# Graph layers on one core: 120 single-row tiles for 116, and the last two blocks normed in turn

## The chip, the cores and the metric

The kernel runs on one core of one Trainium2 chip. The metric is the device time of the whole program in microseconds (us), the median of several runs. One further execution is recorded by the hardware profiler; its own time and its span (first to last instruction of the program) are given beside each other.

## The reference

Two relational graph layers over 12,500 nodes of 128 floats and 200,000 edges sorted by destination, with eight relations, then a layer norm:

```python
W = jnp.einsum('rb,bio->rio', comp, basis)
msgs = einsum('ni,rio->nro', x, W)[src, et]
mean = segment_mean(msgs, dst * 8 + et)          # per node and relation
h = relu(mean.reshape(N, 8, 128).sum(1) + h @ root + bias) + h   # twice
out = layernorm(x + h)
```

## The kernel before

**Tiles.** The edges are cut into 1563 tiles of 128, and eight tiles make an octet: 196 octets per layer, the last with three tiles. The nodes are cut into 98 blocks of 128; the last, block 97, has 84. Blocks are normed in groups of eight, 13 groups; the last group holds the 212 nodes of blocks 96 and 97.

**Gathers and single rows.** For each tile, the 128 source rows are brought into SBUF. Most tiles take one indirect DMA issued by POOL (`gather`, L766). Some tiles, listed in `lists` (L647 to L653), take 128 DMAs of a single row each, issued by SP or ACT (`lone_rows`, L702), in chunks of 32; ahead of each chunk the queue loads 32 row addresses (L697). A list entry gives the queue, the first tile, the bound, the step, the chunk, the lead in octets and the hosts, the SBUF tiles that receive the rows and are used in turn. A chunk is emitted up to 15 octets ahead of its use. SP emits all chunks that are due, ACT at most one per octet.

**Layer 1.** Tables of messages for all nodes and relations lie in HBM as `y_d`. For each octet, in this order, the loop at the end emits the gathers (five octets ahead into seven row buffers), SP's and ACT's single rows, PE's matmuls `add_rows` (each tile's rows against its one-hot matrix, L1451, and for the first octet of a block the root term, L1454), DVE's `onehot` for the octet after next (L1188, two buffers), and one step of `todo`. From octet 190 on, the gather of an octet is emitted only two octets ahead and waits for PE's matmuls of the octet three before it (`LATE`, `after`). The order on each engine is the order of emission; every engine works its list in order, and waits are semaphores that the planner `Plan.add` derives from what is read and written. For a PSUM bank a read counts as a write.

**Blocks.** A block is summed in PSUM over the octets that hold its edges. `finish` adds what the block before it left over (L1360), makes the carry for the next block (L1364), and applies relu and residual into `wide` (L1383), with features on the partitions.

**Norm.** `norm(n)` puts ten steps into `todo`, one per octet: PE turns a group's blocks back to nodes on the partitions (L1511), DVE adds x (L1521) and takes statistics (L1527, L1530), ACT the square root (L1533), DVE the reciprocal (L1537, three octets later) and the scaling (L1540), and SP stores. ACT's square root stands on ACT behind the single-row chunks emitted before it.

**The end.** The last group is loaded as 106 partitions with two nodes each, so both of its slots need both blocks. In the last octet PE first puts x into two PSUM banks (`x_first`, L1485), then the root term (L1468), the carry (L1469) and the three tiles (L1471); then block 97 is finished, and `norm` turns both slots onto x (L1508), takes both statistics, one square root, one reciprocal and both scalings. SP and ACT each store a part. From octet 192 on, all pending norm steps are emitted within their octet.

Of the kernel before, what the change touches and what calls it, by code (L numbers as in the profile page):

```python
# [428 lines left out]
def ordered_path(  # L429
# [209 lines left out]
    def floats(t, n):  # L639
# [5 lines left out]
    mixer_f = mixer.rearrange("p m k -> p (m k)")  # L645
    idx_f = idx.bitcast(F32)
    lists = [  # L647
        [("SP", 90, 1552, 47, 32, 15, [(jmp.bitcast(F32), ["jmp"], []), (comp_sb, ["comp"], []),
                                     (sel.rearrange("p g k -> p (g k)"), ["sel"], [])]),
         ("ACT", 13 * Q + 2, 46 * Q, 8 * Q, 16, 10, [(floats(yr_f, j), yr_cells, yr_cells) for j in range(5)]),  # L650
         ("ACT", 53 * Q + 2, 1552, 8 * Q, 16, 10, [(floats(mixer_f, j), ["mixer"], []) for j in range(2)])],
        [("SP", 62, 1552, 49, 32, 15, [(floats(sT_f[0], j), [("sT", 0, 0), ("sT", 0, 1)], []) for j in range(4)]),
         ("ACT", 65, 1552, 50, 32, 15, [(floats(sT_f[1], j), [("sT", 1, 0), ("sT", 1, 1)], []) for j in range(4)])]]  # L653
    single, at_row = [{}, {}], [0, 0]
    for l in range(L):
        for k, (_, t0, t1, by, _, _, hosts) in enumerate(lists[l]):
# [562 lines left out]
    def in_rows(a, n):  # L1219
        p, k = shape_of(n)  # L1220
        return a[n * GN:n * GN + p * k, :].rearrange("(p s) d -> p (s d)", s=k)

    def load_x(n):
        if n >= NX:
            return
        p, k = shape_of(n)
        t, c = xs[n] = xg_r.take()
        load(t[:p, :k, :].rearrange("p s d -> p (s d)"), in_rows(x, n), [], [c])

    def by_slot(t, n):  # L1230
# [3 lines left out]
    def turn_x(n, h):  # L1234

        p, k = shape_of(n)
        pt, pc = pt_b
        m = min(4, k)

        def first_step():  # L1240
            t, c = xs[n]
            if h == 0:
                xT[n] = wide_r.take()

            def emit():
                for s in range(m):
                    last = nc.tensor.transpose(pt[:, s, :p], t[:p, 4 * h + s, :], ident[:p, :p])
                return last

            pe(emit, [c, "ident"], [pc])  # L1250

        def second_step(copy=copy):
            o, oc = xT[n]
            copy(by_slot(o, n)[:, 4 * h:4 * h + m, :], pt[:, :m, :p], [pc], [oc + (h,)])

        return first_step, second_step
# [175 lines left out]
             (s_b[1][0].rearrange("p t d -> p (t d)")[:, :2 * P], s_b[1][1]),  # L1432
             (ct_b[0].rearrange("p t d -> p (t d)")[:, :2 * P], ct_b[1])]

    def add_rows(q, k, opens, last):
        t, c = rows_g.pop((1, q))
        d, dc = dms.pop((1, q))
        a, ac = acc[k]
        n = in_quad(q)
        root_in = opens and k >= 0  # L1440
        more = []
        if root_in:
            ht, hc = hT[:, k * P:k * P + rows_of(k)], ("h", k)
            more += [hc, ("w", 1, R)]

        lones = lones_of(1, q)

        def some(i0, i1):
            def emit():
                for i in range(i0, i1):  # L1450
                    ins = nc.tensor.matmul(a, lones[i][0] if i in lones else t[:, i, :], d[:, i, :],  # L1451
                                           start=(opens and i == 0), stop=(last and i == n - 1 and q != SOON // Q))
                    if i == 0 and root_in:
                        nc.tensor.matmul(a[:, :rows_of(k)], w_sb[:, 1, R, :], ht, start=False, stop=False)  # L1454
                if q == SOON // Q:
                    ins = nc.tensor.matmul(a, fix_rows, fix_dm, start=False, stop=last)
                return ins

            return emit

        if q == NQ - 2:
            for h in range(2):
                pe(some(4 * h, 4 * h + 4), [c + (h,)] + dc + more, [ac, ("done", 1)])
        elif q == NQ - 1:
            m = rows_of(k)
            assert opens and last and k == NT - 1
            ct, cc = carry.pop(k)
            pe(lambda: nc.tensor.matmul(a[:, :m], w_sb[:, 1, R, :], ht, start=True, stop=False), more, [ac])  # L1468
            pe(lambda: nc.tensor.matmul(a[:, :m], ident, ct[:, :m], start=False, stop=False), [cc, "ident"], [ac])  # L1469
            for i in range(n):  # L1470
                pe(lambda i=i: nc.tensor.matmul(a[:, :m], t[:, i, :], d[:, i, :m], start=False, stop=i == n - 1),  # L1471
                   [c + (i,)] + dc, [ac, ("done", 1)])
        else:
            pe(some(0, n), [c + (0,), c + (1,)] + dc + more + [x for _, cs in lones.values() for x in cs]
               + (fix_rows_c + fix_dm_c if q == SOON // Q else []),
               [ac, ("done", 1)])
        plan.mark("PE")

    def x_first():
        n = NX - 1  # L1480
        p, k = shape_of(n)
        xt, xc = xs[n]
        assert k == 2
        for s, (b, bc) in enumerate(po_b):
            pe(lambda s=s, b=b: nc.tensor.matmul(b[:p, 0, :], ident[:p, :p], xt[:p, s, :], start=True, stop=False),  # L1485
               [xc, "ident"], [bc])

    def norm(n):

        p, k = shape_of(n)  # L1490
        vt, vc = wide[n]
        xt, xc = xs[n]
        st, sc = st_r.take()
        A, M = nc.vector.BN_STATS_DIM, nc.vector.BN_AGGR_DIM
        z = xt[:p]
        on_x = n == NX - 1
        y = [b[:p, 0, :] for b, _ in po_b] if on_x else [z[:, s, :] for s in range(k)]
        yc = [c for _, c in po_b] if on_x else [xc + (0,)]
        halves = [(h, min(4, k - 4 * h)) for h in range(-(-k // 4))]

        def turn():
            for h, m in halves:
                b, bc = po_b[h]

                def emit(h=h, m=m, b=b):
                    for s in range(m):
                        if on_x:
                            last = nc.tensor.matmul(po_b[s][0][:p, 0, :], by_slot(vt, n)[:, s, :], ident,  # L1508
                                                    start=False, stop=True)
                        else:  # L1510
                            last = nc.tensor.transpose(b[:p, s, :], by_slot(vt, n)[:, 4 * h + s, :], ident)  # L1511
                    return last

                pe(emit, [vc + (j,) for j in range(n * S, min(n * S + S, NT))] + ["ident"],
                   [c for _, c in po_b] if on_x else [bc])

        def add():
            for h, m in [] if on_x else halves:
                b, bc = po_b[h]
                zh = z[:, 4 * h:4 * h + m, :]  # L1520
                vec(lambda b=b, m=m, zh=zh: nc.vector.tensor_add(zh, b[:p, :m, :], zh), [bc, xc], [xc + (0,)])  # L1521

        def each(f):
            return in_turn([lambda s=s: f(s) for s in range(k)])

        def stats():
            vec(each(lambda s: nc.vector.bn_stats(st[:p, s, :A], y[s])), yc, [sc + (0,)])  # L1527

        def aggr():
            vec(each(lambda s: nc.vector.bn_aggr(st[:p, s, A:A + M], st[:p, s, :A])), [sc + (0,)], [sc + (1,)])  # L1530

        def root_of():
            act(lambda: nc.scalar.activation(st[:p, :k, A + M], st[:p, :k, A + 1], AF.Sqrt, bias=eps[:p]),  # L1533
                [sc + (1,), "eps"], [sc + (2,)])

        def one_by():
            vec(lambda: nc.vector.reciprocal(st[:p, :k, A + M], st[:p, :k, A + M]), [sc + (2,)], [sc + (3,)])  # L1537

        def scale():
            vec(each(lambda s: nc.vector.tensor_scalar(z[:, s, :], y[s], st[:p, s, A:A + 1], st[:p, s, A + M:],  # L1540
                                                       op0=ALU.subtract, op1=ALU.mult)),
                [sc + (1,), sc + (3,)] + (yc + [xc] if on_x else []), [xc + (0,)])

        def store():
            cut = p // 16 * 16
            for q, p0, p1 in (("SP", 0, cut), ("ACT", cut, p)):
                if p1 > p0:
                    load(in_rows(out, n)[p0:p1], xt[p0:p1, :k, :].rearrange("p s d -> p (s d)"), [xc + (0,)],
                         [("out", n, q)] + ([xc] if p0 == 0 else []), q)

        todo.extend([turn, add, stats, aggr, root_of, lambda: None, lambda: None, one_by, scale, store])
# [223 lines left out]
    for q in range(NQ):  # L1775
# [11 lines left out]
        if opens:  # L1787
            acc[k] = acc_b[k % 3]
        if q == NQ - 1:
            x_first()  # L1790
        add_rows(q, k, opens, last)
        onehot(1, q + 2)
        if todo:
# [1 line left out]
        for i in range(2):  # L1795
            for j, step in ending:
                step()
                n = j // S
                if j >= 0 and (j % S == S - 1 or j == NT - 1):
                    norm(n)  # L1800
                    if n + 2 < NX:
                        todo.extend([lambda: None] * 3 + [lambda n=n: load_x(n + 2)])
            ending.clear()
            if i == 0 and last:
                a, b = finish(1, k)
                a()
                ending.append((k, b))
# [69 lines left out]
```

## Time and profile before

| | |
|---|---|
| median of 3 runs | 3784.03 us (3783.49 to 3790.35) |
| profiled execution | 3783.55 us, span 3781.7 us |
| granted TensorE clock, mean | 0.83 |
| busy: PE / DVE / ACT / POOL | 2413.2 / 1694.7 / 354.0 / 2844.7 us |
| gathers, layer 0 / layer 1 | 1508 / 1502 |
| single-row DMAs, layer 1, SP / ACT | 3968 / 3840 |

Issuing DMAs isn't counted as busy, so ACT's and SP's work on single rows shows in timelines and not in the busy times. A line of a timeline gives start, duration (merged over several instructions where it has a count), engine, line, operation, tiles, count, and in brackets the idle time before it and what ended it. "SPq" and "ACTq" are DMA issues of these engines.

### The profile page before, as it was taken

The page shows a single profiled execution, that of the slowest core. Times are in us where ns is not written, and L with a number is a line of the kernel's source. Part 1 is how long each engine was busy: PE and PEld are TensorE (multiplying, and loading weights), DVE is VectorE, ACT ScalarE, POOL GpSimd, SP SyncE. Part 2 cuts the span into 40 slices and gives each one's busy share as a digit, 9 for nine tenths or more (in the row PEclk, how much of TensorE's full clock was granted, in tenths as well). Part 3 has the DMA queues.
Part 4 walks back from the last instruction along what each step waited for, and adds up shares of the span by engine and source line. Part 5 has one row for each costly group of instructions (what it writes and reads, how often), then busy time and mean ns, then how long its engine had stood idle before and what let it go on. Part 6 is the DMA issues. An engine that isn't in the chain of part 4 may idle for free.

```text
span 3781.7 us, 62930 instructions
## 1 busy us (share of the span) xinstructions
PE 2413.2 (64%) x11367; PEld 1933.4 (51%) x11367; DVE 1694.7 (45%) x4752; ACT 354.0 (9%) x794; POOL 2844.7 (75%) x3019
## 2 busy tenths in 40 slices
PE   5777667777666676777765555556566555655655
PEld 3566645555555555665543444444444444444444
DVE  5556424444333333343344444444444444454444
ACT  1121211211111111111100000000000000000000
POOL 7777777777777777777777777777777777777776
PEclk8999879999888888788888787777777777787778
DMA  4122223433322222223232222222222222222222
GB/s 125 56 62 62 56 92 102 123 111 101 99 87 81 89 89 84 84 82 96 92 85 55 56 62 61 65 63 61 66 56 67 66 56 67 60 62 67 67 54 61
DMA packets 155888, 286.71 MB, mean 76 GB/s; under 512 B 67013, under 2 KB 89474, under 8 KB 155482
## 3 DMA queue, kind: packets, MB, share of 16 engines
q0 software_dynamic: 96352, 197.52, 20.3%
q10 hardware_dynamic: 30461, 55.51, 4.5%
q1 hardware_dynamic: 28669, 29.60, 3.0%
q14 instruction: 314, 2.57, 0.2%
q8 instruction: 92, 1.51, 0.2%
HBM read 223.72 MB, written 58.65 MB: 75 GB/s over the span
## 4 chain that ended last, share of the span: by engine, by line
POOL 52%; issue 19%; DMA 11%; PE 9%; ACTq 4%; ACT 2%; DVE 2%; SPq 2%; POOLq 0%; DVEq 0%
POOL rows L766 52%; DMA rows<-y_d,idy 9%; ACTq L702 3%; PE s L1276 2%; PE s L1451 1%; SPq L702 1%; ACT sT L623 1%; ACTq L697 1%; PE y L1308 1%; DVE dm L1188 1%; PE pt L1406 1%; PE ct L959 1%; PE ct L960 1%; DVE arena L949 1%; PE pt L907 1%
## 5 line engine op out<-in xcount | busy, mean ns | idle before, releaser
L766 POOL DMA_INDIRECT rows<-in_x_dram,idx x1508 | 1425.2, 945 | 462.4 <-issue 455.7
L766 POOL DMA_INDIRECT rows<-y_d,idy x1502 | 1417.4, 944 | 458.5 <-issue 446.9
L1188 DVE TENSOR_SCALAR dm<-cols,near,w 128x256 f32<-128x256 f16 x1563 | 723.8, 534 | 952.1 <-PE s L1451 570.3
L1451 PE MATMUL s<-dm,rows 128*128 128x256 f32 x1984 | 659.9, 495 | 447.7 <-DMA rows<-y_d,idy 349.0
L1451 PEld LDWEIGHTS s<-dm,rows 128*128 128x128 f32 x1984 | 491.9, 257 | 580.2 <-issue 316.9
L1188 DVE TENSOR_SCALAR dm<-cols,kr,w 128x128 f32<-128x128 f16 x1563 | 524.9, 400 | 201.8 <-PE s L1276 177.5
L1276 PEld LDWEIGHTS s<-dm,rows 128*128 128x128 f32 x3016 | 436.3, 225 | 291.7 <-DMA rows<-in_x_dram,idx 243.0
L1276 PE MATMUL s<-dm,rows 128*128 128x128 f32 x3016 | 462.1, 313 | 189.0 <-DMA rows<-in_x_dram,idx 182.3
L1451 PE MATMUL ct<-dm,rows 128*128 128x256 f32 x1014 | 341.9, 501 | 294.2 <-DMA rows<-y_d,idy 281.4
L1451 PEld LDWEIGHTS ct<-dm,rows 128*128 128x128 f32 x1014 | 255.3, 262 | 364.2 <-issue 234.5
L1308 PE MATMUL y<-w_sb,sT 128*128 128x128 f32 x1968 | 270.1, 296 | 55.8 <-ACT sT L623 55.8
L1308 PEld LDWEIGHTS y<-w_sb,sT 128*128 128x128 f32 x1968 | 257.0, 211 | 64.6 <-ACT sT L623 63.6
L1406 PE MATMUL pt<-w_sb,arena 128*128 128x512 f32 (+1 forms) x386 | 222.5, 660 | 62.3 <-DVE y_row L626 42.3
L1339 PE MATMUL po<-pl,ys 128*128 128x256 f32 x392 | 138.4, 437 | 140.8 <-ACT sT L623 135.9
L623 ACT ACTIVATE sT<-s 128x512 f32<-128x512 f32 x391 | 213.5, 606 | 83.7 <-PE s L1276 83.4
L626 DVE COPY y_row<-pt 128x512 f32<-128x512 f32 x56 | 38.7, 691 | 364.6 <-PE pt L1406 364.6
L623 ACT ACTIVATE y_row<-pt 128x512 f32<-128x512 f32 (+1 forms) x139 | 83.0, 597 | 1041.7 <-PE s L1276 574.3
L1308 PE MATMUL ct<-w_sb,sT 128*128 128x128 f32 (+1 forms) x1168 | 159.8, 296 | 0.7 <-ACT sT L623 0.7
L1308 PEld LDWEIGHTS ct<-w_sb,sT 128*128 128x128 f32 (+1 forms) x1168 | 155.0, 213 | 1.3 <-ACT sT L623 1.1
L1533 ACT ACTIVATE st<-st,eps 128x8 f32<-128x8 f32 (+1 forms) x13 | 4.0, 308 | 1586.5 <-DMA sT<-y_d 736.9
L1339 PEld LDWEIGHTS po<-pl,ys 128*128 128x128 f32 x392 | 65.2, 201 | 169.0 <-ACT sT L623 159.0
L1360 DVE TENSOR_TENSOR po<-po,carry 128x128 f32<-128x128 f32 x98 | 29.0, 296 | 263.8 <-PE s L1276 242.7
(210 smaller groups left out, 1296.9 us busy)
## 6 DMA issues: line engine op xcount, KB each, us to landing
sT<-y_d SPq DMA_DIRECT2D x3968, 0.5 KB
sT<-y_d ACTq DMA_DIRECT2D x3840, 0.5 KB
y_d<-y_row ACTq DMA_DIRECT2D x96, 512.0 KB
mixer<-in_x_dram ACTq DMA_DIRECT2D x2304, 0.5 KB
rows<-in_x_dram,idx POOLq DMA_INDIRECT x1508
rows<-y_d,idy POOLq DMA_INDIRECT x1502
jmp<-in_x_dram SPq DMA_DIRECT2D x1408, 0.5 KB
comp_sb<-in_x_dram SPq DMA_DIRECT2D x1408, 0.5 KB
```

Of the source, the lines that this page charges most:

```text
L623: act(lambda: nc.scalar.activation(out_t, in_t, AF.Copy), reads, writes)
L626: vec(lambda: nc.vector.tensor_copy(out_t, in_t), reads, writes)
L697: _, at = nc.values_load_multi_w_load_instructions(offs[r:r + 1, l * P + j * ch:l * P + (j + 1) * ch], engines=[mybir.EngineType.SP if e = ...
L702: return [eng.dma_start(o[j * ch + i:j * ch + i + 1, :].bitcast(byte), table_b[bass.ds(v, 4 * D)].rearrange("(p d) -> p d", p=1)) for i, v ...
L766: ins.append(nc.gpsimd.indirect_dma_start(out=t[:, i - q * Q, :], out_offset=None, in_=table_t, in_offset=bass.IndirectOffsetOnAxis(ap=ids ...
L907: last = nc.tensor.matmul(pt[:, b, :], t[:, b, :], m, start=(i == 0), stop=(i == len(parts) - 1))
L1188: emits.append(lambda i=i: nc.vector.tensor_scalar(t[:, i - q * Q, :wide], cols[:, :wide], ids[:, i:i + 1], w[:, i:i + 1], op0=ALU.is_equa ...
L1276: last = nc.tensor.matmul(s_b[i // 4][0][:, i % 4, :], lones[i][0] if i in lones else t[:, i, :], d[:, i, :], start=True, stop=True)
L1308: last = nc.tensor.matmul(y[:m], t[:, r, :nt, :].rearrange("p t k -> p (t k)"), w_sb[:, 0, r, :], start=(r == 0), stop=(r == R - 1))
L1339: ins = nc.tensor.matmul(a, o[:m], t[:m], start=opens, stop=last and not root_in)
L1406: pe(lambda: nc.tensor.matmul(hb[:n].rearrange("p r d -> p (r d)"), hT[:, j * P:j * P + n], w_sb[:, 1, k * H:(k + 1) * H, :].rearrange("p ...
L1451: ins = nc.tensor.matmul(a, lones[i][0] if i in lones else t[:, i, :], d[:, i, :], start=(opens and i == 0), stop=(last and i == n - 1 and ...
```

## The change

- The lists of single-row tiles have other starts and steps: layer 0, SP from tile 91 every 45 (before: 90 every 47); layer 1, SP every 47 (49) and ACT from tile 63 every 48 (65 every 50).
- The last group's two slots are its two blocks: block 96 on 128 partitions, block 97 on 84. x for it is loaded by two DMAs, and turned and copied per block.
- Ahead of octet 194, PE puts x of both blocks into PSUM and the root term of block 97 into its bank (`first_sums`). In octet 195 PE sums tiles 0 and 1, turns block 96 onto x, adds the carry and sums tile 2.
- Block 96 is finished in the order add, relu and residual, carry. The two blocks are normed by `last_norm`, one after the other, their steps interleaved on DVE; block 96 is stored by SP, block 97 by ACT.

```diff
-        [("SP", 90, 1552, 47, 32, 15, [(jmp.bitcast(F32), ["jmp"], []), (comp_sb, ["comp"], []),
+        [("SP", 91, 1552, 45, 32, 15, [(jmp.bitcast(F32), ["jmp"], []), (comp_sb, ["comp"], []),
...
-        [("SP", 62, 1552, 49, 32, 15, [(floats(sT_f[0], j), [("sT", 0, 0), ("sT", 0, 1)], []) for j in range(4)]),
-         ("ACT", 65, 1552, 50, 32, 15, [(floats(sT_f[1], j), [("sT", 1, 0), ("sT", 1, 1)], []) for j in range(4)])]]
+        [("SP", 62, 1552, 47, 32, 15, [(floats(sT_f[0], j), [("sT", 0, 0), ("sT", 0, 1)], []) for j in range(4)]),
+         ("ACT", 63, 1552, 48, 32, 15, [(floats(sT_f[1], j), [("sT", 1, 0), ("sT", 1, 1)], []) for j in range(4)])]]
...
+        if n == NX - 1:
+            for s, (j, p) in enumerate(ends_at):
+                load(t[:p, s, :], x[j * P:j * P + p, :], [], [c])
+            return
...
-            pe(lambda: nc.tensor.matmul(a[:, :m], w_sb[:, 1, R, :], ht, start=True, stop=False), more, [ac])
-            pe(lambda: nc.tensor.matmul(a[:, :m], ident, ct[:, :m], start=False, stop=False), [cc, "ident"], [ac])
             for i in range(n):
+                if i == n - 1:
+                    between_last()
+                    pe(lambda: nc.tensor.matmul(a[:, :m], ident, ct[:, :m], start=False, stop=False),
+                       [cc, "ident"], [ac])
                 pe(lambda i=i: nc.tensor.matmul(a[:, :m], t[:, i, :], d[:, i, :m], start=False, stop=i == n - 1),
...
+    def first_sums():
+        xt, xc = xs[NX - 1]
+        for i, ((_, p), (b, bc)) in enumerate(zip(ends_at, po_b)):
+            pe(lambda i=i, p=p, b=b: nc.tensor.matmul(b[:p, 0, :], ident[:p, :p], xt[:p, i, :], start=True, stop=False),
                [xc, "ident"], [bc])
+        k = NT - 1
+        a, ac = acc[k] = acc_b[k % 3]
+        m = rows_of(k)
+        pe(lambda: nc.tensor.matmul(a[:, :m], w_sb[:, 1, R, :], hT[:, k * P:k * P + m], start=True, stop=False),
+           [("h", k), ("w", 1, R)], [ac])
...
+    def last_norm(i):
...
+        def turn():
+            pe(lambda: nc.tensor.matmul(y, vt[:, i * P:i * P + p], ident, start=False, stop=True),
+               [vc + (j,), "ident"], [bc])
+        def stats():
+            vec(lambda: nc.vector.bn_stats(t[:, :A], y), [bc], [sc + (i, 0)])
+            vec(lambda: nc.vector.bn_aggr(t[:, A:A + M], t[:, :A]), [sc + (i, 0)], [sc + (i, 1)])
+            act(lambda: nc.scalar.activation(t[:, A + M:], t[:, A + 1:A + 2], AF.Sqrt, bias=eps[:p]),
+                [sc + (i, 1), "eps"], [sc + (i, 2)])
+        def one_by():
+            vec(lambda: nc.vector.reciprocal(t[:, A + M:], t[:, A + M:]), [sc + (i, 2)], [sc + (i, 3)])
+        def scale():
+            vec(lambda: nc.vector.tensor_scalar(z, y, t[:, A:A + 1], t[:, A + M:], op0=ALU.subtract, op1=ALU.mult),
+                [sc + (i, 1), sc + (i, 3), bc, xc], [xc + (i,)])
+            load(out[j * P:j * P + p, :], z, [xc + (i,)], [("out", NX - 1, i)], ("SP", "ACT")[i])
...
         if q == NQ - 1:
-            x_first()
+            last_st = st_r.take()
+            turn, stats, one_by, scale = zip(*(last_norm(i) for i in range(2)))
+            add_rows(q, k, opens, last, turn[0])
+            stats[0]()
+            for step in finish(1, k):
+                step()
+            turn[1]()
+            one_by[0]()
+            stats[1]()
+            scale[0]()
+            one_by[1]()
+            scale[1]()
+            break
+        if q == NQ - 2:
+            first_sums()
         add_rows(q, k, opens, last)
...
-            if i == 0 and last:
+            if q == NQ - 2:
+                if i == 0:
+                    for step in finish(1, k, True):
+                        step()
+            elif i == 0 and last:
```

More of the change, by code (lines that the diff above doesn't have):

```diff
@@ L1221, in in_rows @@
         return a[n * GN:n * GN + p * k, :].rearrange("(p s) d -> p (s d)", s=k)
+    ends_at = [(j, rows_of(j)) for j in range((NX - 1) * S, NT)]
+    assert len(ends_at) == 2
     def load_x(n):
@@ L1246, in emit @@
                 for s in range(m):
-                    last = nc.tensor.transpose(pt[:, s, :p], t[:p, 4 * h + s, :], ident[:p, :p])
+                    r = ends_at[s][1] if n == NX - 1 else p
+                    last = nc.tensor.transpose(pt[:, s, :r], t[:r, 4 * h + s, :], ident[:r, :r])
                 return last
@@ L1253, in second_step @@
             o, oc = xT[n]
+            if n == NX - 1:
+                for s, (_, r) in enumerate(ends_at):
+                    copy(o[:, s * P:s * P + r], pt[:, s, :r], [pc], [oc + (s,)])
+                return
             copy(by_slot(o, n)[:, 4 * h:4 * h + m, :], pt[:, :m, :p], [pc], [oc + (h,)])
@@ L1433, in ordered_path, with add_rows @@
              (ct_b[0].rearrange("p t d -> p (t d)")[:, :2 * P], ct_b[1])]
-    def add_rows(q, k, opens, last):
+    def add_rows(q, k, opens, last, between_last=None):
         t, c = rows_g.pop((1, q))
@@ L1477, in add_rows @@
         plan.mark("PE")
[L1479 to L1485, printed above, removed]
-               [xc, "ident"], [bc])
+    def first_sums():
+        xt, xc = xs[NX - 1]
+        for i, ((_, p), (b, bc)) in enumerate(zip(ends_at, po_b)):
+            pe(lambda i=i, p=p, b=b: nc.tensor.matmul(b[:p, 0, :], ident[:p, :p], xt[:p, i, :], start=True, stop=False),
+               [xc, "ident"], [bc])
+        k = NT - 1
[4 more added lines that the diff above has]
+    def last_norm(i):
+        j, p = ends_at[i]
+        xt, xc = xs[NX - 1]
+        vt, vc = wide[NX - 1]
+        st, sc = last_st
+        b, bc = po_b[i]
+        y, z = b[:p, 0, :], xt[:p, i, :]
+        A, M = nc.vector.BN_STATS_DIM, nc.vector.BN_AGGR_DIM
+        t = st[:p, i, :]
+        def turn():
[12 more added lines that the diff above has]
+            load(out[j * P:j * P + p, :], z, [xc + (i,)], [("out", NX - 1, i)], ("SP", "ACT")[i])
+        return turn, stats, one_by, scale
     def norm(n):
@@ L1495, in norm @@
         z = xt[:p]
-        on_x = n == NX - 1
-        y = [b[:p, 0, :] for b, _ in po_b] if on_x else [z[:, s, :] for s in range(k)]
-        yc = [c for _, c in po_b] if on_x else [xc + (0,)]
         halves = [(h, min(4, k - 4 * h)) for h in range(-(-k // 4))]
@@ L1506, in emit @@
                     for s in range(m):
[L1507 to L1511, printed above, removed]
-                    return last
-                pe(emit, [vc + (j,) for j in range(n * S, min(n * S + S, NT))] + ["ident"],
-                   [c for _, c in po_b] if on_x else [bc])
+                        last = nc.tensor.transpose(b[:p, s, :], by_slot(vt, n)[:, 4 * h + s, :], ident)
+                    return last
+                pe(emit, [vc + (j,) for j in range(n * S, min(n * S + S, NT))] + ["ident"], [bc])
         def add():
-            for h, m in [] if on_x else halves:
+            for h, m in halves:
                 b, bc = po_b[h]
@@ L1526, in stats @@
         def stats():
-            vec(each(lambda s: nc.vector.bn_stats(st[:p, s, :A], y[s])), yc, [sc + (0,)])
+            vec(each(lambda s: nc.vector.bn_stats(st[:p, s, :A], z[:, s, :])), [xc + (0,)], [sc + (0,)])
         def aggr():
@@ L1539, in scale @@
         def scale():
-            vec(each(lambda s: nc.vector.tensor_scalar(z[:, s, :], y[s], st[:p, s, A:A + 1], st[:p, s, A + M:],
+            vec(each(lambda s: nc.vector.tensor_scalar(z[:, s, :], z[:, s, :], st[:p, s, A:A + 1], st[:p, s, A + M:],
                                                        op0=ALU.subtract, op1=ALU.mult)),
-                [sc + (1,), sc + (3,)] + (yc + [xc] if on_x else []), [xc + (0,)])
+                [sc + (1,), sc + (3,)], [xc + (0,)])
         def store():
@@ L1798, in ordered_path @@
                 n = j // S
-                if j >= 0 and (j % S == S - 1 or j == NT - 1):
+                if j >= 0 and j % S == S - 1:
                     norm(n)
```

## The prediction

> **What bounds the kernel now.** I read the chain of waits first, then the source view of the gather line, then the timelines of the queues that the moved rows go to, and last the tail.
>
> ```profile
> span 3781.7 us, 62930 instructions
> POOL 52%; issue 19%; DMA 11%; PE 9%; ACTq 4%; ACT 2%; DVE 2%; SPq 2%; POOLq 0%; DVEq 0%
> L766 POOL DMA_INDIRECT rows<-in_x_dram,idx x1508: 940/944/1177, 4.6 to 1888.9; - x189
> L766 POOL DMA_INDIRECT rows<-y_d,idy x1502: 940/944/1009, 1890.2 to 3768.1; - x188
>   issue: 902.6, 2957
>   PE s L1451: 3.4, 11
> ```
>
> POOL starts its first gather at 4.6 and its last at 3768.1, and the two layers follow each other without a gap (1888.9, then 1890.2). That is 3010 gathers in 3763.5 us, 1.250 us each: 0.944 busy, the rest almost all "issue" (902.6 us over 2957 gathers, 0.305 each). Waits for another engine are hardly there (3.4 us for PE). So POOL is the bound and a gather is worth 1.25 us. This holds as long as what POOL waits for stays early, and two things can make it late: the row buffers, and the last six octets, whose gathers are held until PE has done the octet three before.
>
> **Part 1: four gathers less.** The ranges in the lists give 33 + 5 + 18 = 56 single-row tiles in layer 0 (55 before) and 32 + 32 = 64 in layer 1 (61 before). So the change does what it says: one gather less in layer 0, three in layer 1. The first moves the start of layer 1, the others its end, one for one: 4 x 1.250 = 5.0 us. The nearest row with another price is busy time alone, 0.944: 3.8 us. I take 5.0, since "issue" goes away with its gather.
>
> **Part 2: what the 4 x 128 rows cost on the queues.** In layer 1 both queues are in the way of other work, ACT above all, because the square root of every normalisation (L1533) stands in its order behind 32-row chunks.
>
> ```profile
> 1913.76 269.62 ACTq L702 DMA_DIRECT2D sT<-y_d  x640
> 2183.40 1.28 ACT L1533 ACT_TABLE_LOAD   x1 [277.08 <-DMA sT<-y_d]
> L702 ACTq DMA_DIRECT2D sT<-y_d x1344: 231/240/584, 2199.9 to 2799.3; - x192
> 2469.83 156.59 ACTq L702 DMA_DIRECT2D sT<-y_d  x352
> 2773.06 150.01 ACTq L702 DMA_DIRECT2D sT<-y_d  x352
> 3211.08 137.95 ACTq L702 DMA_DIRECT2D sT<-y_d  x320
> 3362.38 130.62 ACTq L702 DMA_DIRECT2D sT<-y_d  x320
> 3522.62 102.46 ACTq L702 DMA_DIRECT2D sT<-y_d  x256
> 3661.18 0.31 ACT L1533 ACTIVATE st<-st,eps 128x8 f32<-128x8 f32 x1 [140.54 <-DVE dm L1188]
> 2185.04 0.21 DVE L1537 RECIPROCAL st<-st 128x8 f32<-128x8 f32 x1 [15.35 <-ACT st L1533]
> 2340.52 0.20 DVE L1537 RECIPROCAL st<-st 128x8 f32<-128x8 f32 x1 [24.78 <-ACT st L1533]
> ```
>
> ACT issues without a pause: 640 DMAs are 20 chunks in 269.62 us, 13.5 us each. From 2199.9 to 2799.3 it is 42 chunks in 599.4, 14.3 each with the square roots between them. Later, with about 2.3 us added for the gap after each square root: 152.3/11 = 13.8, 140.3/10 = 14.0, 132.9/10 = 13.3, 104.8/8 = 13.1. So ACT is late early on, and DVE's reciprocal waits 15.35 and 24.78 us for it at the first two normalisations. Before the end it has caught up: at 3661.18 ACT waited for DVE, not the reverse.
>
> With a tile every 48 instead of every 50, ACT never catches up. I count chunks in emission order. Ahead of the first square root are 21 (20 now), ahead of the second 32 (31), ahead of the eleventh, that of blocks 80 to 87, all 128 (120 now). The eleventh is reached at 1913.76 - 1.25 + 269.62 x 21/20 + 1.3 = 2196.9, plus 107 chunks. At 42 x 14.3 + 65 x 13.7 (the four later rates have a mean of 13.6) that is 2196.9 + 600.6 + 890.5 = 3688; with 14.0 for the last 65, the slower of those rates, 3707. I take both as the ends of the likely case.
>
> ```profile
> 3688.65 0.20 DVE L1537 RECIPROCAL st<-st 128x8 f32<-128x8 f32 x1
> 3694.90 3.71 DVE L1188 TENSOR_SCALAR dm<-cols,near,w 128x256 f32<-128x256 f16 x8 [5.85 <-PE ct L1451]
> 3709.55 5.38 PE L1451 MATMUL s<-dm,rows 128*128 128x256 f32 x16 [4.36 <-DMA rows<-y_d,idy]
> 3768.10 0.94 POOL L766 DMA_INDIRECT rows<-y_d,idy  x1 [0.31 <-issue]
> ```
>
> DVE will ask for it at 3688.65 - 5 = 3683.7, so it waits some 5 to 24 us. Queued behind it on DVE is the one-hot of octet 188 (3.71 us), behind that PE's 16 passes of that octet (5.38), and behind PE's octet 188 stand POOL's gathers of octet 191, one of the last six. These start naturally 33 gathers before the last: 3768.1 - 5.0 - 33 x 1.249 = 3721.9. So the square root may come as late as 3721.9 - 5.4 - 3.7 - about 0.8 of hops = 3712 and cost nothing; past that, POOL loses one for one. My 3688 to 3707 lies 5 to 24 us inside. The earlier waits are longer (about 40 us at the second) but there POOL runs ahead into seven row buffers, and PE normally trails it by under two octets: some five octets of (3768.1 - 1890.2)/195 = 9.6 us, 48 us of cover, besides the two one-hots that DVE has built before it waits. I cost them at nothing; without that cover each would cost its excess. The rows themselves come in time: the last tile ACT loads (1551, octet 193) is issued before 3707, and that octet's matmuls come after 3750.
>
> SP has more room: its 128 rows take about 53 us (below, 768 in 317.10) against 45 gathers of 1.25 = 56. In layer 0 its list is also still shorter than its period, and nothing stalls. The last group of x is loaded by two DMAs to one cell, so the second waits on SP for the first, twice in the kernel, a few us each, with no row due behind it.
>
> ```profile
> 1913.58 317.10 SPq L702 DMA_DIRECT2D sT<-y_d  x768
> ```
>
> **Part 3: the tail.** In order of time:
>
> ```profile
> 3764.36 3.31 DMA rows<-y_d,idy
> 3767.71 3.55 PE L1451 MATMUL s<-dm,rows 128*128 128x256 f32 x8 [2.53 <-DMA rows<-y_d,idy]
> 3771.05 0.77 PE L1485 MATMUL po<-x_g,ident 106*106 106x128 f32 x4
> 3771.29 0.30 DVE L1360 TENSOR_TENSOR s<-s,carry 128x128 f32<-128x128 f32 x1 [5.71 <-PE s L1451]
> 3771.66 0.35 PE L1468 MATMUL s<-arena,w_sb 128*128 128x84 f32 x2
> 3771.88 0.29 DVE L1383 SCALAR_TENSOR_TENSOR wide<-s,arena 128x128 f32<-128x128 f32 x1
> 3771.90 0.45 PE L1469 MATMUL s<-carry,ident 128*128 128x84 f32 x2
> 3772.19 0.83 PE L1471 MATMUL s<-dm,rows 128*128 128x84 f32 x6
> 3773.06 0.24 DVE L1383 SCALAR_TENSOR_TENSOR wide<-s,arena 128x84 f32<-128x84 f32 x1 [0.89 <-PE s L1471]
> 3773.36 0.69 PE L1508 MATMUL po<-ident,wide 128*106 128x128 f32 x4 [0.34 <-DVE wide L1383]
> 3774.09 0.50 DVE L1527 BATCH_NORM_STATS2 st<-po 106x6 f32<-106x128 f32 x2 [0.78 <-PE po L1508]
> 3774.62 0.25 DVE L1530 BATCH_NORM_AGGREGATE st<-st 106x2 f32<-106x6 f32 x2
> 3774.90 0.30 ACT L1533 ACTIVATE st<-st,eps 106x2 f32<-106x2 f32 x1 [13.09 <-DVE st L1530]
> 3775.23 0.17 DVE L1537 RECIPROCAL st<-st 106x2 f32<-106x2 f32 x1 [0.37 <-ACT st L1533]
> 3775.44 0.73 DVE L1540 TENSOR_SCALAR x_g<-po,st 106x128 f32<-106x128 f32 x2
> 3776.20 0.34 ACTq L620 DMA_DIRECT2D out_dram<-x_g  x1
> ```
>
> The x and root passes (0.77 + 0.35) go to PE's idle time of 2.53 us before 3767.71: free. But the last pass does not come 1.1 us earlier, because the carry now comes after the relu of block 96 on DVE. On today's clock: add 3771.29, relu to 3771.92, carry to 3772.3; block 96 into PSUM 3771.98 to 3772.35; carry pass, last tile's passes, to 3772.98. Now it is 3773.02: nothing gained. From there one block is normed instead of two slots: relu 0.24, one slot's pass 0.36, stats 0.27, aggregate 0.20, root 0.30, reciprocal 0.17, scale 0.38, seven hops of about 0.03: 2.15, against 3776.20 - 3773.02 = 3.18. Block 96's own stats and scale lie in DVE's waits for PE and ACT. Gain about 1.0 us; none if they do not fit there (they are 0.27 + 0.20 + 0.17 + 0.38 = 1.0), 1.3 if DVE's instructions overlap more. The last store and what follows it, 3781.7 - 3776.2 = 5.5, stays.
>
> **The sum.** The profiled execution took 3783.55 us (span 3781.7). 3783.55 - 5.0 - 1.0 = 3777.55. The median of the runs shown, 3784.03, is 0.48 above it: 3778.0, or 0.16% less. About 0.2% (7.6 us: 3776.5 to 3791.6) is what a measurement of this kernel can tell from no change.
>
> **The rivals.**
> - *ACT's square root becomes the bound.* If the pace of 2469.83 ((156.59 + 2.3)/11 = 14.44 a chunk) lasts the whole layer, the eleventh is reached at 2196.9 + 107 x 14.44 = 3742, 30 us past 3712, and POOL stands for them at octet 191: 3808, slower. It decides from 14.16 a chunk on; each 0.1 beyond costs 10.7. For it: the stretch to 2799 held 14.3, and the two lists are now denser. Against: the first 20 chunks and all after 2773 were quicker. The Trainium skill ("DMA: Bandwidth & Descriptors", section "Issuing engines are not separate DMA queues") says that DMAs of the scalar, sync and gpsimd engines run on the same 16 DMA engines and interleave; by that rule the added rows hinder each other and the gathers, which speaks for this rival, and DMA_DIRECT2D's spread of 231/240/584 ns agrees.
> - *The same, mildly:* 14.16 to 14.29 a chunk, up to 13 us lost: 3779 to 3791, no change.
> - *The tail gains nothing* (block 96's steps push block 97's): 3779.0, no change.
> - *More than counted:* 1.3 in the tail and a quieter DMA side: 3776, just faster.
>
> **How the numbers follow.** Forecast, with the tail as summed or without gain (3776.5 to 3779.5): 0.68. Mild delay: 0.12. ACT the bound by more than 13 us: 0.12. More than counted: 0.08. The range reaches from 3775.7 (1.3 in the tail, and a run's scatter of 1) to 3789, which takes in most of the mild delay. Faster 0.08, same 0.80, slower 0.12.
>
> **What would show it.** Right: 1507 and 1499 gathers in the gather line, the last starting near 3763.1 with no wait on PE; DVE's reciprocals waiting 20 to 45 us for ACT in the first half and less at the eleventh; the last out store some 6 us earlier. Wrong: a gap of POOL in the 3720s released by PE, with the eleventh square root after 3712; or a tail in which block 97's statistics wait for block 96's scale.

## The result and the profile after

Over 20 runs each, the changed kernel takes 3776.43 us in the median (3775.01 to 3778.68), the kernel before 3783.14: 6.7 us less, a ratio of 0.9984 with a 95% interval of 0.9978 to 0.9990. That lies inside the range of 3775.7 to 3789 and within the 0.2% counted as no change, though the interval is narrow enough to say that it is a little faster.

The page of after (its span, and the shares of the chain):

```profile
span 3774.6 us, 63987 instructions
POOL 41%; issue 17%; DMA 14%; PE 9%; ACTq 8%; SPq 4%; ACT 3%; DVE 2%; POOLq 0%; DVEq 0%
```

and the gather line in its source view, with POOL's idle time by "issue" below:

```profile
L766 POOL DMA_INDIRECT rows<-in_x_dram,idx x1507: 940/944/1264, 4.7 to 1887.4; - x189
L766 POOL DMA_INDIRECT rows<-y_d,idy x1499: 940/944/1047, 1888.7 to 3762.4; - x188
  issue: 899.1, 2945
```

3006 gathers for 3010, at the same busy time and the same "issue" each. The last starts at 3762.4 instead of 3768.1: 5.7 us, of which four gathers are 5.0. The chain now has ACTq and SPq at 8% and 4% (4% and 2% before) and POOL at 41% (52%): POOL still sets the pace, but the queues with the single rows now lie on the chain for part of the time.

The timelines of ACT and of DVE, around the normalisations (the first two lines are the second, the others the eleventh):

```profile
2350.10 0.31 ACT L1571 ACTIVATE st<-st,eps 128x8 f32<-128x8 f32 x1 [154.78 <-DMA sT<-y_d]
2350.44 0.21 DVE L1575 RECIPROCAL st<-st 128x8 f32<-128x8 f32 x1 [34.91 <-ACT st L1571]
3694.79 3.71 DVE L1188 TENSOR_SCALAR dm<-cols,near,w 128x256 f32<-128x256 f16 x8 [6.46 <-PE ct L1463]
3705.12 0.31 ACT L1571 ACTIVATE st<-st,eps 128x8 f32<-128x8 f32 x1 [158.54 <-DMA sT<-y_d]
3705.46 0.21 DVE L1575 RECIPROCAL st<-st 128x8 f32<-128x8 f32 x1 [6.97 <-ACT st L1571]
```

The eleventh square root came at 3705.12, directly behind ACT's own row issues. In the waits of the whole span (total, number, longest), DVE's reciprocal waits 244.9 us for ACT in 12 waits; before it was 40.9 in 4. The idle time of POOL has no wait for PE above 0.3 us, the length of its usual gap:

```profile
POOL rows L766 <- issue: 899.1, 2945, 0.3
POOL rows L766 <- PE s L1463: 1.5, 5, 0.3
DVE st L1575 <- ACT st L1571: 244.9, 12, 34.9
```

The tail, in order of time:

```profile
3762.41 0.94 POOL L766 DMA_INDIRECT rows<-y_d,idy  x1 [0.30 <-issue]
3764.94 0.30 DVE L1372 TENSOR_TENSOR s<-s,carry 128x128 f32<-128x128 f32 x1 [2.13 <-PE s L1463]
3765.28 0.29 DVE L1395 SCALAR_TENSOR_TENSOR wide<-s,arena 128x128 f32<-128x128 f32 x1
3765.60 0.35 DVE L1402 TENSOR_SCALAR carry<-s,bias_t 128x128 f32<-128x128 f32 x1
3765.62 0.49 PE L1515 MATMUL po<-ident,wide 128*128 128x128 f32 x2 [0.31 <-DVE wide L1395]
3766.30 0.39 PE L1485 MATMUL s<-dm,rows 128*128 128x84 f32 x2
3766.72 0.25 DVE L1395 SCALAR_TENSOR_TENSOR wide<-s,arena 128x84 f32<-128x84 f32 x1
3767.51 0.29 DVE L1519 BATCH_NORM_STATS2 st<-po 84x6 f32<-84x128 f32 x1 [0.32 <-PE po L1515]
3767.84 0.18 DVE L1520 BATCH_NORM_AGGREGATE st<-st 84x2 f32<-84x6 f32 x1
3767.94 0.38 DVE L1528 TENSOR_SCALAR x_g<-po,st 128x128 f32<-128x128 f32 x1
3768.05 0.29 ACT L1521 ACTIVATE st<-st,eps 84x1 f32<-84x1 f32 x1 [1.06 <-DVE st L1520]
3769.01 0.35 ACTq L620 DMA_DIRECT2D out_dram<-x_g  x1
```

From the last gather's start to the last store's issue it is 6.60 us, before 8.10. Block 96's scaling (3767.94) lies beside block 97's square root, as the change's order on DVE intends. From the store to the end it is 5.6 us (5.5 before).

### The profile page after: what moved, and what is told of

Read it like the earlier page. It is cut to its first block, busy times and chain, and to the rows that moved or that the text cites. A ratio compares the mean times of both kernels' runs of the same rounds, so it can differ in the third digit from the quotient of the medians.

```text
span 3774.6 us, 63987 instructions
## 1 busy us (share of the span) xinstructions
PE 2394.9 (63%) x11367; PEld 1919.0 (51%) x11367; DVE 1692.9 (45%) x4754; ACT 354.4 (9%) x795; POOL 2840.8 (75%) x3015
## 4 chain that ended last, share of the span: by engine, by line
POOL 41%; issue 17%; DMA 14%; PE 9%; ACTq 8%; SPq 4%; ACT 3%; DVE 2%; POOLq 0%; DVEq 0%
POOL rows L766 41%; DMA rows<-y_d,idy 12%; ACTq L702 6%; SPq L702 4%; ACTq L697 2%; PE s L1288 2%; ACT sT L623 2%; PE y L1320 1%; PE pt L1418 1%; ACT y_row L623 1%; SPq L697 1%; PE s L1463 1%; DVE dm L1188 1%; PE ct L959 1%; PE ct L960 1%
## 5 line engine op out<-in xcount | busy, mean ns | idle before, releaser
L1463 PE MATMUL s<-dm,rows 128*128 128x256 f32 x1984 | 627.9, 478 | 444.7 <-DMA rows<-y_d,idy 328.2
L1463 PEld LDWEIGHTS s<-dm,rows 128*128 128x128 f32 x1984 | 472.5, 247 | 569.9 <-issue 305.8
L1288 PEld LDWEIGHTS s<-dm,rows 128*128 128x128 f32 x3014 | 435.9, 225 | 273.6 <-DMA rows<-in_x_dram,idx 222.7
L1463 PE MATMUL ct<-dm,rows 128*128 128x256 f32 x1008 | 357.4, 521 | 305.0 <-DMA rows<-y_d,idy 190.1
L1463 PEld LDWEIGHTS ct<-dm,rows 128*128 128x128 f32 x1008 | 265.7, 274 | 379.2 <-issue 202.8
```

The costliest lines, as they stand in the source:

```text
L1288: last = nc.tensor.matmul(s_b[i // 4][0][:, i % 4, :], lones[i][0] if i in lones else t[:, i, :], d[:, i, :], start=True, stop=True)
```

## The experiments

**A series on a chip where the queues are slow.** The first four kernels ran together, beside the kernel before, on a chip on which the kernel before itself took 5790.47 us. There was no other series on that chip, so whether the chip or the moment was slow is not shown.

Lists alone: the kernel before with

```diff
-        [("SP", 90, 1552, 47, ...
+        [("SP", 91, 1552, 45, ...
...
-        [("SP", 62, 1552, 49, ...
-         ("ACT", 65, 1552, 50, ...
+        [("SP", 62, 1552, 47, ...
+         ("ACT", 63, 1552, 48, ...
```

> The kernel before with the new lists of single-row tiles alone; its tail is the old one. Theory (a gather of POOL is worth 1.25 us, ACT's lateness stays hidden): 4 x 1.25 = 5.0 us under the kernel before, 3778.1, last gather starting near 3763, DVE's reciprocals waiting about 245 us in all for ACT as in the changed kernel. Rival 1 (the gain is the tail's): 3783, no change. Rival 2 (the added rows slow the gathers too, so less than 1.25 each): 3779 to 3782.

Tail alone: the changed kernel with these three entries as before.

> The changed kernel with the old lists of single-row tiles; only the tail is new. Theory: last gather at 3768 as before, and from there to the last store's issue about 6.6 instead of 8.1 us, of which about 0.9 is the norm and the rest PE's clock in octet 194 (chance): 1.0 us under the kernel before, 3782.1. Rival (the tail gives the whole 1.5): 3781.6. Rival 2 (the tail gives the whole change): 3776.4.

Sums late: `first_sums()` moved from ahead of octet 194 to the start of octet 195.

```diff
         if q == NQ - 1:
...
+            first_sums()
             add_rows(q, k, opens, last, turn[0])
...
-        if q == NQ - 2:
-            first_sums()
```

> The changed kernel, but x and the root term enter PSUM in the last octet, after octet 194, as before the change. Theory: PE's 1.1 us then stand between octet 194 and the last tiles, where PE otherwise waits about 0.5 us for DVE's relu: 0.6 us over the changed kernel, 3777.0. Rival 1 (the carry on DVE sets the end anyway): 3776.4. Rival 2 (all of it counts): 3777.5.

Reciprocal later:

```diff
-        todo.extend([turn, add, stats, aggr, root_of, lambda: None, lambda: None, one_by, scale, store])
+        todo.extend([turn, add, stats, aggr, root_of, lambda: None, lambda: None, lambda: None, lambda: None, lambda: None, one_by, scale, store])
...
-                        todo.extend([lambda: None] * 3 + [lambda n=n: load_x(n + 2)])
+                        todo.extend([lambda: None] * 2 + [lambda n=n: load_x(n + 2)])
```

> The changed kernel with the reciprocal of each norm put five instead of two octets after the square root (and the load of x one octet earlier after the store). Theory (DVE's 245 us of waits for ACT are hidden by the row buffers): the waits fall by some 20 to 29 us each, to under 60 in all, and the time does not move, 3776.4 within 1 us. Rival (part of these waits reaches the end): faster by 2 us or more.

| kernel | median | ratio to the kernel before |
|---|---|---|
| lists alone | 5925.49 | 1.0232 (1.0203 to 1.0261) |
| tail alone | 5782.61 | 0.9990 (0.9972 to 1.0008) |
| sums late | 5926.34 | 1.0243 (1.0216 to 1.0270) |
| reciprocal later | 5922.05 | 1.0230 (1.0208 to 1.0252) |

None of the four expectations fits. All three with the new lists are 2.3 to 2.4% slower, the one with the old lists is not. Lists alone, the chain on its page:

```profile
SPq 60%; issue 35%; another core or an unknown queue 2%; PE 1%; DVE 1%; ACTq 1%; DMA 0%; ACT 0%; DVEq 0%
```

the gather line of layer 0 in the source view, with what POOL waited for in both layers:

```profile
L766 POOL DMA_INDIRECT rows<-in_x_dram,idx x1507: 938/944/1157, 4.7 to 2809.9; - x189
  PE s L1276: 746.7, 80
  PE s L1451: 520.3, 21
  PE ct L1451: 474.4, 16
```

what PE waited for in layer 1, in the waits view:

```profile
PE ct L1451 <- DMA sT<-y_d: 709.5, 15, 56.8
PE s L1451 <- DMA sT<-y_d: 660.5, 15, 54.6
```

the rows of SP:

```profile
L702 SPq DMA_DIRECT2D sT<-y_d x4096: 2/228/1407, 2863.6 to 5860.6; - x196
L702 SPq MOVE sT<-y_d x4096: 2/29/1412, 2863.5 to 5860.5; - x196
```

and the same rows of SP in the changed kernel on the usual chip:

```profile
L702 SPq DMA_DIRECT2D sT<-y_d x4096: 224/228/623, 1911.3 to 3696.9; - x196
L702 SPq MOVE sT<-y_d x4096: 29/29/29, 1911.3 to 3696.8; - x196
```

There SP takes (5860.6 - 2863.6)/4096 = 0.73 us for a row of layer 1, and in the changed kernel on the usual chip 0.44 by the same quotient. Medians of the single instructions are equal, but even a register move of 29 ns takes up to 1412. So SP is the bound, POOL waits for PE and PE for rows, and a tile given to SP costs 128 x 0.73 = 94 us in layer 1 instead of saving 1.25. Tail alone, with the old lists, has SPq at 59% and issue at 36% of its chain on that chip, so SP bounds the old lists there too. The new lists give SP one tile more in each layer. In layer 0 a row took (2792.0 - 123.4)/4224 = 0.63 us, so that tile is 81; with the 94 of layer 1 that makes 175 us. 135 came out. By the last gathers of the two traces (2727.9 and 5766.0 with tail alone, 2809.9 and 5900.1 with lists alone), layer 0 took 82 us more and layer 1 only 52; why less there is not shown. Why the queues pause was not studied.

**The same four on a usual chip**, again in one series; there the kernel before took 3781.80.

> The same kernel as rows_only (old tail, new lists), measured again beside the kernel before. If the kernel before takes about 3783 us, POOL is the bound and the theory says 4 x 1.25 = 5.0 us less, 3778. If it takes about 5790 us again, SP is the bound (two more SP tiles of some 94 us of issue each, less what was slack) and it is again some 2.3% slower. Rival: the sign depends on something else than which engine is the bound, so the slower ratio shows up at 3783 us too.

> The same kernel as tail_only (new tail, old lists), measured again. At about 3783 us for the kernel before: 0.9 to 1.5 us less, 3781.5 to 3782.1, by the theory; 3776.4 by the rival that the tail gives all.

> The same kernel as sums_late (x and root term after octet 194), measured again. At about 3783 us for the kernel before: 0.6 us over the changed kernel's 3776.4 by the theory (0.4 to 0.8), none by the rival that the carry sets the end, 1.1 by the rival that all of PE's passes count.

> The same kernel as recip_late (reciprocal five octets after the square root), measured again. At about 3783 us for the kernel before: 3776.4 within 1 us by the theory that the row buffers hide DVE's waits; 2 us or more under that by the rival. late11_far, with the same order and 40 us more on ACT, took 3774.6 in one run, which leans to a small gain.

| kernel | median (lowest to highest) | ratio to the kernel before |
|---|---|---|
| lists alone | 3778.04 (3774.67 to 3780.10) | 0.9989 (0.9980 to 0.9998) |
| tail alone | 3780.37 (3779.49 to 3781.93) | 0.9996 (0.9987 to 1.0005) |
| sums late | 3776.86 (3774.85 to 3780.30) | 0.9987 (0.9978 to 0.9996) |
| reciprocal later | 3775.17 (3773.46 to 3778.70) | 0.9983 (0.9974 to 0.9992) |

Lists alone give 3.8 us, with an interval from 0.8 to 7.6 that has the 5.0 inside; the rival that the tail gives it all falls, and so does a slower sign on a usual chip. Its profiled run stood at 3776.49, 5.3 under the kernel before, with the last gather at 3761.8, so the 5.0 can be had; what its slower runs lose no trace shows. Tail alone gives 1.4, not resolved by its interval. For sums late the interval doesn't separate 3776.86 from the changed kernel; no verdict. In its trace the last gather is followed by the last store 8.7 us later, but PE's passes were slow there too.

Two of these traces show a loss that was not in the sum. POOL stands for PE at the gathers of the last six octets, first in sums late, then in lists alone:

```profile
3712.39 0.94 POOL L766 DMA_INDIRECT rows<-y_d,idy  x1 [2.87 <-PE s L1463]
3720.53 0.94 POOL L766 DMA_INDIRECT rows<-y_d,idy  x1 [0.92 <-PE s L1451]
```

The eleventh square root had come at 3703.49 and 3704.07 there, earlier than in the changed kernel, where POOL did not stand. So it was not the square root but PE, which was late for another reason; the section on the prediction returns to it.

Reciprocal later has the waits of DVE for ACT at

```profile
DVE st L1575 <- ACT st L1571: 19.1, 5, 12.9
```

against 244.9, and a ratio of 0.9983 against the changed kernel's 0.9984. So some 226 us of waiting of DVE were worth nothing that can be measured. The two intervals together leave room for about 4 us, so a gain of 2 us, the rival, is not excluded.

**Where ACT's lateness begins to count.** Idle work on ACT ahead of one square root, one run of each kernel; the kernel before took 3782.53 beside them.

```diff
         def root_of():
+            if n == 10:                                  # second kernel: n == 1
+                idle = yr_r.tiles[0].rearrange("p r d -> p (r d)")
+                for _ in range(36):
+                    act(lambda: nc.scalar.activation(idle, idle, AF.Sqrt, bias=eps, scale=0.0), [], yr_cells)
```

> The changed kernel with 36 idle activations of 128x1024 on ACT ahead of the eleventh square root, about 40 us (they write a buffer that nothing reads any more). Theory: in the changed kernel that square root came at 3705 and could have come at 3712 for nothing; at 3745 POOL stands about 33 us ahead of octet 191's gathers, 3809. Rival (the waits of DVE do not reach POOL): 3776.

3810.11 us. The timelines of ACT, DVE and POOL:

```profile
3702.82 42.45 ACT L1574 ACTIVATE y_row<-y_row,eps 128x1024 f32<-128x1024 f32 x36 [155.38 <-DMA sT<-y_d]
3745.18 0.29 ACT L1575 ACTIVATE st<-st,eps 128x8 f32<-128x8 f32 x1
3745.51 0.20 DVE L1579 RECIPROCAL st<-st 128x8 f32<-128x8 f32 x1 [45.09 <-ACT st L1575]
3755.69 0.94 POOL L766 DMA_INDIRECT rows<-y_d,idy  x1 [34.26 <-PE s L1463]
```

ACT is 40 us late, POOL stands 34.26 us once, 33.96 more than the usual gap, and resumes 10.5 after the square root. So 3745.18 - 33.96 = 3711.2 is where it begins to count; 3712 was forecast. The changed kernel's 3705.12 is 6 us inside.

> The same 36 activations ahead of the second square root. Theory: ACT has no pause in which to recover, so the 40 us are still there at the eleventh; the second reciprocal waits about 75 us, more than buffers and one-hots cover, so POOL stands some 10 to 20 us near octet 50 and for the rest of about 33 us at octet 191: 3800 to 3809 again. Rival 1 (hidden by the buffers and recovered over the layer): 3776. Rival 2 (each place costs its own excess): 3825.

3800.96 us. The second square root and its reciprocal, POOL, and the eleventh square root:

```profile
2394.19 0.29 ACT L1575 ACTIVATE st<-st,eps 128x8 f32<-128x8 f32 x1
2394.51 0.21 DVE L1579 RECIPROCAL st<-st 128x8 f32<-128x8 f32 x1 [77.98 <-ACT st L1575]
2405.26 0.94 POOL L766 DMA_INDIRECT rows<-y_d,idy  x1 [24.50 <-PE s L1463]
3730.02 0.31 ACT L1575 ACTIVATE st<-st,eps 128x8 f32<-128x8 f32 x1 [154.63 <-DMA sT<-y_d]
```

The time was right and its split wrong. POOL stands 24.5 us at once, more than the 10 to 20 expected, and no more near the end. Everything behind is 24 us later, and the eleventh square root at 3730.02 is only 25 us later than in the changed kernel: ACT made up 15 of its 40 us, which I had held impossible. Both rivals fall: it isn't hidden, and the places don't add up. Of DVE's wait of 77.98 us, POOL felt 24.50 - 0.30 = 24.2, so 53.8 were covered; the prediction had 48 for the row buffers, and the two one-hots besides.

> The 36 activations ahead of the eleventh square root and the reciprocal five octets after it. Theory: the gate is the distance from the square root to the last six octets' gathers: with the reciprocal behind the one-hot of octet 190, the first octet held back is 191, and the gathers behind it are those of 194, some 27 us later; POOL stands 0 to 6 us: 3776 to 3783. Rival (ACT's 40 us count wherever the reciprocal stands): 3809.

3774.61 us, no wait of POOL near the end. But the test is weaker than meant: in this order ACT reached the idle work at 3682.72 instead of 3702.82, so the square root came at 3725.09. In the old order that would have cost 3725.1 - 3711.2 = 14 us; here it cost none. The rival of 3809 falls.

```diff
-         ("ACT", 63, 1552, 48,
+         ("ACT", 61, 1552, 46,
```

> The changed kernel with ACT's tiles from 61 every 46: 33 tiles for 32, one gather less (132 chunks of rows, all ahead of the eleventh square root). Theory: 4 chunks of about 13.95 us more put that square root near 3760, 48 past 3712: POOL stands 25 to 49 us in all, 3800 to 3824. Rival (a gather less is 1.25 us less): 3775.

3808.41 us, inside the expected 3800 to 3824, with POOL's waits for PE at

```profile
  PE s L1463: 25.6, 9
  PE ct L1463: 13.6, 6
```

But they stand at other places than expected:

```profile
2692.58 0.21 DVE L1575 RECIPROCAL st<-st 128x8 f32<-128x8 f32 x1 [69.35 <-ACT st L1571]
2703.54 0.94 POOL L766 DMA_INDIRECT rows<-y_d,idy  x1 [18.45 <-PE s L1463]
3479.73 0.94 POOL L766 DMA_INDIRECT rows<-y_d,idy  x1 [12.12 <-PE ct L1463]
3743.15 0.31 ACT L1571 ACTIVATE st<-st,eps 128x8 f32<-128x8 f32 x1 [138.75 <-DMA sT<-y_d]
3752.96 0.94 POOL L766 DMA_INDIRECT rows<-y_d,idy  x1 [5.03 <-PE s L1463]
```

The eleventh square root came at 3743.15 instead of the expected 3760, and POOL lost only 5 us behind it. The other 30 went at the fourth and the ninth square root, where DVE's reciprocals waited 69.35 and 69.22 us for ACT, more than was covered (69.35 - 18.15 = 51.2, and 57.4 at the ninth). So the time was right and its place wrong: the limit that this tile passes first is that of the early waits, at 51 to 57 us, and the changed kernel's longest wait, 34.91, is some 16 us inside it. One tile more on ACT saves a gather and loses 32 us: ACT's queue is full. No version here beats the changed kernel by more than the measurement tells.

## Why the prediction was right

- **Four gathers, 5.0 us.** 5.7 in the trace, with the price of a gather unchanged; lists alone gave 3.8 in the median, between 0.8 and 7.6 by its interval. The mechanism is right and the traces have its size; the runs alone would not settle it.
- **ACT's square root: late, not too late.** Forecast for the eleventh 3688 to 3707, measured 3705.12; limit forecast 3712, measured 3711.2; waits of DVE at the second about 40, measured 34.91, and at the eleventh 5 to 24, measured 6.97. The rival ("ACT becomes the bound") is real and 6 us away, as the idle work showed. That it stayed away is in part luck. From the first square root (2195.01) to the eleventh it is (3705.12 - 2195.01)/107 = 14.11 us a chunk, at the slow end of the likely case, and with the measured limit the rival begins at (3711.2 - 2195.01)/107 = 14.17; the rates from which the forecast was made spread from 13.1 to 14.4. The early waits, costed at nothing, cost nothing: the longest was 34.91 and 51 to 57 were covered.
- **A step that failed, with little harm.** I had DVE ask for the eleventh square root at 3683.7, today's time less 5. It asked at 3694.79 + 3.71 = 3698.5. The one-hot ahead of that reciprocal, in the kernel before, came at

```profile
3685.03 3.71 DVE L1188 TENSOR_SCALAR dm<-cols,near,w 128x256 f32<-128x256 f16 x8 [3.80 <-PE ct L1451]
```

with the tail alone at

```profile
3682.48 3.71 DVE L1188 TENSOR_SCALAR dm<-cols,near,w 128x256 f32<-128x256 f16 x8 [3.08 <-PE ct L1463]
```

  and with the new lists at 3694.79, though POOL is 5.7 us earlier. It waits for PE, and PE for gathered rows: from the last gather of the octet that PE works on to this one-hot it is 8.0 us in the kernel before and 6.5 with the tail alone, but 22.4 with the new lists, some 15 more. That DVE's waits for ACT had made PE late would be another explanation. It falls: with the reciprocal later, where those waits are 19.1 us in all, the same one-hot comes at

```profile
3692.66 3.71 DVE L1188 TENSOR_SCALAR dm<-cols,near,w 128x256 f32<-128x256 f16 x8 [9.23 <-PE ct L1463]
```

  21.9 us behind its octet's last gather. In the kernel before, the single rows were all issued by 3633; now they run to 3705. And the kernel before has the same lag while its own rows are issued: 20.3 us in the mean of octets 120 to 149, and 8.4 in that of octets 180 to 189. So gathered rows are later at PE while single rows are issued, which I had not in the sum. The DMA records agree: between 3645 and 3690, in the mean, 34.8 of the 4-byte packets that close a gather (16 to each) are due and not finished in the changed kernel, and 25.5 in the kernel before. This lateness of PE made the eleventh wait short, not the margin long, and it is what POOL stood for, 2.87 and 0.92 us, in sums late and lists alone. The Trainium skill ("DMA: Bandwidth & Descriptors", section "Issuing engines are not separate DMA queues") says that DMAs of the scalar, sync and gpsimd engines (ACT, SP and POOL here) run on the same 16 DMA engines and interleave; the traces agree, in that the lag of some 15 us stands only while single rows are issued. That sharing is the cause is argued, not shown.
- **The tail, 1.0 us.** Right in its sign; its size stays open: 1.5 between these two traces, and 1.4 in the runs, which their interval does not resolve. Of the terms, the norm came out close (from the add of octet 194 to the store 4.07 us, before 4.91, so 0.84). The rest, 0.66, is octet 194's second half: 8 passes took 3.55 us before, and here they ended 2.0 us after they were released. The granted clock, in the windows view (stretch, ..., PEclk, DMA share, GB/s), differed there; the kernel before:

```profile
3767.00:3771.30 4.30, 3.59 (x10) 2.88 (x11) 0.01 (x1) 0.00 (x0) 1.74 (x2) 0.61 0.20 52
```

and after:

```profile
3761.00:3765.00 4.00, 4.00 (x22) 3.29 (x21) 1.87 (x6) 0.00 (x0) 1.88 (x2) 1.00 0.58 181
```

  That part need not belong to the change: in the trace of lists alone, with the old tail, these 8 passes took 1.99 us. Over all traces on a usual chip, from the last gather's start to the last store's issue, the old tail takes 8.1 and 7.4 us (two traces) and the new one 5.7 to 6.7 (seven traces, sums late not counted), so one pair of executions can show from 0.7 to 2.4.
- **The rivals.** The tail without gain fell by the traces; neither the mild nor the heavy delay by ACT occurred in the changed kernel, and the idle work showed that a delay by ACT can occur. The chance of 0.12 for "slower" missed what did make it slower elsewhere: SP, not ACT, in the series where the queues were slow.

## What to carry to other kernels

Work moved from a bound engine to a queue with room is worth its full price only until something else in that queue's order gets late: find the last instruction that stands behind the moved work, and the time up to which it may come. Waits of an engine that is not the bound can grow sixfold and cost nothing; measure the margin by making the suspect later on purpose. Then look where the bound engine stands, and not only at the time: there were two limits here, one for the early waits and one for the last, and the kernels with the idle work at the second square root and with the 33rd tile took the time expected of them, but lost more of it at the early limit than expected. And a split between two engines that is tuned to within a few us holds for the conditions in which it was tuned: the same lists gained 0.1% in one series and cost 2.3% in another.

## What the runs showed of the hardware

- ACT issues 32 single rows in 13.1 to 14.4 us (layer 1 of the kernel before, by stretches); the pace changes over the layer without a change in the code.
- In one series, on one chip, a row from SP took 0.73 us instead of 0.44, and register moves of 29 ns took up to 1412, while POOL's gather kept its 944 ns.
- With single rows being issued, PE trailed POOL's gathers by 22 us, and without by 6.5 to 8, at the same place in the program (octet 185).
- Seven row buffers and two one-hots let DVE wait 51 to 57 us for ACT in mid-layer before POOL stood still.
